# Column bias from raw weight rows on TensorE, a pinned order of loads and splits, and 40 early transposes, in the first pair of a two-block attention kernel

## The chip, the cores and the metric

The kernel runs on one core of one Trainium2 chip. A core has a matrix engine (TensorE, "PE" in the profile, its weight loads "PEld"), three engines for elementwise work (VectorE "DVE", ScalarE "ACT", GpSimd "POOL"), and DMA engines that move data between memory and the core. All transfers of this kernel are issued by SyncE, in whose rows they stand as "SPq" or "SP". Each engine works through a queue of its own in a fixed order, and waits at its head until what it needs is there.

The metric is the device time of one execution, in microseconds (us).

## The reference, cut to what matters

The inputs are x and a context, both (16, 256, 512) in float32, and a boolean mask (16, 256, 256). Two transformer blocks follow one another. Only the first one is touched:

```python
xq  = layer_norm(x, qn_w, qn_b)
ctx = layer_norm(context, cn_w, cn_b)
q  = (xq @ q_w).reshape(B, N, H, D)             # H = 16 heads of D = 32
kv = (ctx @ kv_w).reshape(B, M, 2, H, D)
k, v = (kv[:, :, 0], kv[:, :, 1])
attn = jnp.einsum('bnhd,bmhd->bhnm', q, k) * scale
attn = softmax(where(xa_mask[:, None], neg, attn))
out = jnp.einsum('bhnm,bmhd->bnhd', attn, v).reshape(B, N, C)
x = x + (out @ proj_w + proj_b)
x = x + gelu(layer_norm(x, n2_w, n2_b) @ fc1_w + fc1_b) @ fc2_w + fc2_b
```

The second block is a causal self-attention, a cross-attention over the same context, and an MLP with ReLU, each followed by a layer norm.

A layer norm ahead of a product splits in two: the product of the normalized input with the weights scaled by the gain, and a constant row, offset times weight, which is the bias of that product. This bias is what the first part of the change computes in another way.

## The kernel before

**Tiles.** The 16 batch items go in 8 pairs; a pair has 4 tiles of 128 rows, 512 rows together. Products of the first block's attention use a rounded 32-bit type. To keep float32 accuracy, every operand is split in a high and a low half (`split`, L119: ACT makes the high half by a rounding copy, DVE the difference), and each product is three matmuls (`mm3`, L255): high by high, high by low, low by high.

**The first phase** (`phase1`, L554). For each pair g, `feed(g)` (L679) makes q, k and v. While it does this for pair g, the stream of score products, exponentials, transposes and value products of the pair before is woven in (`weave`, L330). For pair 0 there is nothing to weave with: `feed(0)` runs alone, and the attention of pair 0 starts behind it.

What `feed(0)` does, in its program order:
1. `normal` (L653) loads four tiles of x (`xin`) and normalizes them: DVE's statistics (L238 to L241), POOL's power for the reciprocal deviation `rstd` (L242), DVE's normalization (L247).
2. `cvec` (gains and offsets), `n2` and `b_fc1` (vectors for the later MLP) are loaded, L688 to L690.
3. `load("q")` (L567) loads four 128-row chunks of q_w as raw rows (`wst`), splits each in `q_w_h` and `q_w_l` (L193, L194), and weighs the raw rows: `by_k` is the sum of the chunks, each times its offsets (`weigh`, L216: POOL multiplies the first, ACT scales the others in place at L222, POOL adds them at L223).
4. `front` (L659) transposes each tile by TensorE (`transposed`, L273) and splits it into `x_t`.
5. Four projections `project_t` (L295) give the four 128-column chunks of q. After the first, `shift` (L203) sums `by_k` over its partitions by four matmuls with a column of ones (`sum_cols`, L226) and copies the bias `q_w_b` out of its bank. Each chunk is split with that bias into the tile `qk` (one buffer, `halves`, L539), and `keep` (L375) stores it to a scratch `d` in memory (L378). Between the projections come the fronts of the context, `c_t`, as `FRONTS` says: tiles 0 and 1 after the first, 2 after the second, 3 after the third.
6. The same for k, with `load("k")`, and fronts of pair 1's x between; then `load("v")`, two tiles of v (`values`), v's bias, and `load_o` (L583): proj_w in four chunks, its constant row by the same weighing with v's bias, and `b_o`.

Raw rows and the attention's transposed probabilities share six buffers under the tag "pts". Matmul results use three banks under "mm"; scores use two ("sc"), transposed probabilities two ("pt"), value products one ("z").

**The attention of a pair** begins (`begin`, L604) with the masks: pair 0 loads its own `mk` (`load_mask`, L613) and POOL converts it to `mb` in four instructions (`mask`, L619); it also loads pair 1's. `build` (L383) loads stacks of q and k for four heads from the scratch, `scores` (L404) makes two products for a head and DVE adds mask and row minimum into `e` (L423), ACT exponentiates (L433), and `turn` (L443) transposes `e` three heads later. `residual` (L667) adds the projection of the result to x, which it loads once more (`xr`, L673), together with `b_o`.

**What sets the order.** TensorE's queue keeps the order in which the program is written (L1534). The queues of DVE, ACT, POOL and SP are put in order by a planner: it models when each instruction can run, and may put later-written instructions ahead of earlier ones when data and buffers allow. Therefore the profile shows some loads of `load_o`, `begin` and `residual` among the first ones issued.

Of the kernel before, what the change touches and what calls it, by code (L numbers as in the profile page):

```python
# [20 lines left out]
P = 128  # L21
# [20 lines left out]
def kernel(ctx: ExitStack, tc: tile.TileContext, a, out):  # L42
# [75 lines left out]

    def split(src, dst, bias=None, scale=None):  # L119
# [11 lines left out]
        else:  # L131
            nc.scalar.copy(dst[0], src)
            nc.vector.tensor_tensor(dst[1], src, dst[0].bitcast(F32), ALU.subtract)
# [10 lines left out]
    class Weight:  # L144
# [30 lines left out]
        def load(self, ks, x0=0, n=C):  # L175

            at = slice(x0, x0 + n)
            for k in ks:
                h, l = self.w[0][:, k, at], self.w[1][:, k, at]
                raw = self.stage()  # L180
                nc.sync.dma_start(
                    out=raw, in_=a[self.name][ts(k, P), self.c0 + x0 : self.c0 + x0 + n]
                )
                self.raw[k] = raw
                if self.gain is None:
                    if self.pooled:
                        nc.gpsimd.tensor_copy(h, raw)
                    else:
                        nc.scalar.copy(h, raw)
                    nc.gpsimd.tensor_tensor(out=l, in0=raw, in1=h.bitcast(F32), op=ALU.subtract)  # L190
                else:
                    by = self.gain[:, k : k + 1]
                    nc.scalar.activation(h, raw, AF.Identity, scale=by)  # L193
                    nc.vector.scalar_tensor_tensor(  # L194
                        l, raw, by, h.bitcast(F32), ALU.mult, ALU.subtract
                    )
        def weigh(self, pool):

            self.by_k = None
            for k, raw in self.raw.items():  # L200
                self.by_k = weigh(pool, self.by_k, raw, self.offset[:, k : k + 1])

        def shift(self):  # L203
            by_k = self.by_k
            if self.form == "row":
                self.b = bank("mm", "ps_b")
                nc.tensor.matmul(self.b, ones.to_broadcast([P, P]), by_k, start=True, stop=True)
            else:
                sum_cols(self.b, by_k)
# [5 lines left out]

    def weigh(pool, total, raw, offset):  # L216

        if total is None:
            total = pool.tile([P, 512], F32, tag="by_k", name="by_k", bufs=1)
            nc.gpsimd.tensor_scalar(total, raw, offset, None, ALU.mult)  # L220
        else:
# [332 lines left out]
    def phase1():  # L554
# [124 lines left out]
        def feed(g):  # L679
# [4 lines left out]
            if g < NG:  # L684
# [20 lines left out]
                if g == 0:  # L705
                    load("k")
# [887 lines left out]
```

## Time and profile before

| what | value |
|---|---|
| median of 6 runs | 2814.69 us |
| lowest and highest run | 2807.13 and 2824.4 us |
| profiled execution | 2816.57 us |
| its span, first to last instruction | 2814.9 us |
| mean granted TensorE clock | 0.982 |
| 0 to 110 us: TensorE busy | 89.44 us |
| 110 to 1000 us: TensorE busy | 859.52 us of 890 |

A page shows busy times of each engine and, in tenths, 40 equal slices of the span. A window row gives the length, the busy time of each engine with its count of instructions, the clock granted to TensorE as a share of full speed, the busy share of the DMA engines, and what they moved in GB/s. A timeline row gives start, length, engine, line, operation, result and operands, and a count; the square brackets say how long the engine had been idle before it and what ended that. Lines are those of the kernel before.

### The profile page before, as it was taken

To read this page: it belongs to the slowest core of one execution; us is meant where nothing else is said; L and a number is where in the kernel's file an instruction comes from. 1 tells how busy PE (TensorE), PEld (TensorE's weight loads), DVE (VectorE), ACT (ScalarE), POOL (GpSimd) and SP (SyncE) were. 2 spreads that over 40 slices of the span, in tenths; PEclk is the share of its full clock that TensorE was granted. 3 is DMA by queue.
4 is the path that set the end of the run, shared out by engine and by line. 5 is a ranking of instruction groups with operands and counts; after the bars stand their busy time and mean duration, and the time that the engine had idled before them with its cause. 6 is when DMAs were issued, how large, how long until landed. Compare 5 with 4: busy or idle time off the path is not lost.

```text
span 2814.9 us, 56659 instructions
## 1 busy us (share of the span) xinstructions
PE 2681.3 (95%) x18970; PEld 2263.5 (80%) x18970; DVE 2050.0 (73%) x5763; ACT 1824.2 (65%) x5292; POOL 864.2 (31%) x874
## 2 busy tenths in 40 slices
PE   7999999998899999999999999999999999999998
PEld 5777777776799999898987877777777777777787
DVE  7666666757646559888876777777777777777887
ACT  4877777778455555444447787877777777777532
POOL 6122221204501127666660111114322212213333
PEclk9999999999899999999999999999999999999999
DMA  6566555644323344434366565567665655555221
GB/s 230 173 194 186 168 181 170 195 157 130 131 106 135 121 147 168 150 120 150 120 207 212 187 188 186 183 191 214 207 192 185 181 184 182 183 171 179 97 91 60
DMA packets 287809, 465.41 MB, mean 165 GB/s; under 512 B 36256, under 2 KB 188320, under 8 KB 279328
## 3 DMA queue, kind: packets, MB, share of 16 engines
q1 hardware_dynamic: 287520, 461.78, 51.1%
q8 instruction: 153, 2.51, 0.4%
q14 instruction: 136, 1.11, 0.1%
HBM read 284.97 MB, written 176.69 MB: 164 GB/s over the span
## 4 chain that ended last, share of the span: by engine, by line
PE 68%; DVE 15%; DMA 7%; issue 4%; POOL 3%; ACT 3%; SPq 1%; POOLq 0%; DVEq 0%; ACTq 0%
PE ps_p L258 18%; PE ps_v L258 14%; PE ps_pt L449 9%; PE ps_s L408 5%; PE ps_z L468 5%; PE down L1015 5%; PE up_sc L902 3%; DVE c_t L142 3%; PE up_pt L902 2%; PE up_mm L902 2%; PE ps_t L277 2%; DVE st L238 1%; DMA xd<-x 1%; DVE e L423 1%; ACT e L433 1%
## 5 line engine op out<-in xcount | busy, mean ns | idle before, releaser
L433 ACT ACTIVATE e<-e,mn 128x256 f32<-128x256 f32 (+1 forms) x1024 | 487.6, 481 | 65.2 <-DVE mn L423 62.8
L455 ACT COPY pt<-ps_pt 128x512 f32<-128x512 f32 (+1 forms) x696 | 378.6, 547 | 181.2 <-PE ps_pt L449 167.8
L449 PE MATMUL ps_pt<-ident,e 128*128 128x128 f32 x2816 | 438.3, 274 | 23.0 <-DVE lbias L1255 11.3
L449 PEld LDWEIGHTS ps_pt<-ident,e 128*128 128x128 f32 x2816 | 337.6, 141 | 63.9 <-ACT pt L455 7.7
L408 PE MATMUL ps_s<-stack 97*128 97x256 f32 (+1 forms) x1536 | 332.5, 298 | 17.1 <-ACT e L433 9.7
L408 PEld LDWEIGHTS ps_s<-stack 97*128 97x128 f32 (+1 forms) x1536 | 269.9, 191 | 76.8 <-ACT e L433 17.4
L1322 POOL TENSOR_TENSOR x<-x,zz 128x256 f32<-128x256 f32 x128 | 95.7, 748 | 731.1 <-DVE zz L1315 673.8
L1015 PE MATMUL down<-w_h,c_t 128*128 128x256 f32 x900 | 263.6, 294 | 22.3 <-DVE c_t L142 22.3
L433 ACT ACTIVATE e<-ps_s,mn 128x256 f32<-128x256 f32 x512 | 241.5, 484 | 58.3 <-DVE mn L419 45.7
L1015 PE MATMUL down<-w_h,x_t 128*128 128x256 f32 x868 | 254.2, 293 | 9.6 <-ACT x_t L141 7.3
L1015 PE MATMUL down<-w_l,x_t 128*128 128x256 f32 x868 | 253.0, 291 | 0.0
L423 DVE CUSTOM_DVE_ANT_0 e<-mb,ps_s 128x256 f32<-128x256 bf16 x512 | 193.1, 416 | 81.3 <-PE ps_s L408 78.9
L242 POOL TENSOR_TENSOR rstd<-rstd,nhalf 128x1 f32<-128x1 f32 x192 | 141.3, 741 | 314.4 <-DVE rstd L241 312.9
L258 PE MATMUL ps_p<-x_t,q_h 128*128 128x512 f32 x640 | 215.5, 417 | 4.2 <-DVE qk L128 2.1
L419 DVE TENSOR_REDUCE mn<-ps_s 128x2 f32<-128x512 f32 x256 | 175.1, 684 | 48.5 <-PE ps_s L408 46.3
L468 PE MATMUL ps_z<-pt,v 128*32 128x256 f32 (+1 forms) x3072 | 199.4, 371 | 3.4 <-DVE pt L453 3.3
L1015 PEld LDWEIGHTS down<-w_h,c_t 128*128 128x128 f32 x900 | 180.4, 201 | 25.7 <-DVE c_t L142 25.7
L423 DVE CUSTOM_DVE_ANT_0 e<-tri,ps_s 128x128 f32<-128x128 f32 (+1 forms) x512 | 160.2, 346 | 53.8 <-PE ps_s L408 51.7
L433 ACT ACTIVATION_READ_ACCUMULATOR e<-e,mn 128x1 f32 x1024 | 197.8, 193 | 0.0
L1015 PEld LDWEIGHTS down<-w_h,x_t 128*128 128x128 f32 x868 | 174.6, 201 | 11.3 <-ACT x_t L141 8.8
L141 ACT CAST x_t<-sums 128x512 fp32r<-128x512 f32 x156 | 92.4, 618 | 136.3 <-DVE sums L791 85.8
L1015 PEld LDWEIGHTS down<-w_l,x_t 128*128 128x128 f32 x868 | 174.5, 201 | 0.0
(245 smaller groups left out, 7478.7 us busy)
## 6 DMA issues: line engine op xcount, KB each, us to landing
stack<-d SPq DMA_DIRECT2D x1152, 128.0 KB
d<-qk SPq DMA_DIRECT2D x192, 512.0 KB
hid<-ho SPq DMA_DIRECT2D x32, 1024.0 KB
raw<-hid SPq DMA_DIRECT2D x32, 1024.0 KB
x<-xd SPq DMA_DIRECT2D x128, 256.0 KB
xd<-x SPq DMA_DIRECT2D x96, 256.0 KB
xin<-in_x_dram SPq DMA_DIRECT2D x32, 256.0 KB
xin<-in_ctx_dram SPq DMA_DIRECT2D x32, 256.0 KB
```

The costliest lines, as they stand in the source:

```text
L242: nc.gpsimd.tensor_tensor(out=rstd[:, 1:2], in0=rstd[:, 0:1], in1=nhalf, op=ALU.pow)
L258: nc.tensor.matmul(ps, w[p], x[q], start=(k == 0 and i == 0), stop=(k == kc - 1 and i == 2))
L408: nc.tensor.matmul(ps[:, t, :], u.st[: self.rows, 0, j, ts(t, P)], u.st[: self.rows, 1, j, :], start=True, stop=True,)
L419: nc.vector.tensor_reduce(mn, ps, AX.X, ALU.min)
L423: nc.vector.tensor_tensor_reduce(out=e[:, at], in0=bias[t], in1=ps[:, t, : job.width[t]], scale=-SC, scalar=BIG, op0=ALU.add, op1=ALU.min, ...
L433: nc.scalar.activation(e[:, at], ps[:, t, :] if bias is None else e[:, at], AF.Exp, bias=mn[:, t : t + 1], scale=-1.0, accum_out=u.rs[:, t ...
L449: nc.tensor.transpose(pp[:, ts(x, P)], e[:, at : at + P], ident)
L455: nc.scalar.copy(pt[:, :n], pp[:, :n])
L468: nc.tensor.matmul(z[ts(j, D), w[0] * P :], job.v[u.i * NT + mc][:, u.c * P + j * D : u.c * P + (j + 1) * D], u.pt[j][:, x0 * P : (x0 + le ...
L902: nc.tensor.matmul(ps[:, mm, :], w[p][:, k, :], x[q][:, k, :], start=(first and mm == k == j == 0), stop=(k == 1 and j == 2), skip_group_c ...
L1015: nc.tensor.matmul(ps[:, t, :], x[p][:, mm, ts(t, P)], w[r][:, bo, :], start=(q == mm == t == j == 0), stop=(q == self.NS - 1 and mm == 1 ...
L1322: nc.gpsimd.tensor_tensor(out=xv, in0=xv, in1=zz, op=ALU.add)
```

## The change

It has four parts, all of them in the first phase, and nearly all in what `feed(0)` issues.

- *Transposes of the identity.* 40 transposes of the identity matrix into a bank that nothing uses yet, at the head of TensorE's queue.
- *Bias of q, k and v.* `sum_cols` and the weighing by POOL and ACT are gone. `shift` makes 16 products instead: each 128 by 128 block of raw rows as the stationary operand by the offset column of its chunk, accumulated over the four chunks. They need only the raw rows and `cvec`. For proj_w, whose bias is a row, the weighing stays and is now done by DVE (one multiplication, three multiply-adds).
- *Order of loads and splits of pair 0.* All four chunks of q_w are loaded ahead; the first is split before the fronts of x, the other three only after the last split of x. The fronts of the context are issued only after that and one projection later (tiles 0 and 1 after the second projection, 2 after the third, 3 after the fourth). `load("k")` comes after the last split of x. `load("v")` moves up, from behind the last k projection to behind the first.
- *Loads kept in program order.* For `b_o`, the masks of pairs 0 and 1, and pair 0's `xr`, the planner may no longer issue the load ahead of earlier-written ones. The loads of `n2` and `b_fc1` move from the start of `feed(0)` to `load_o` and are kept there likewise.

As built, TensorE's order changes only by the 40 transposes, the bias products (16 for 4, three times) and the place of the context's transposes. On SP the masks of pair 0 and 1 now stand behind the last chunks of proj_w, `b_o`, `n2` and `b_fc1`. On DVE the four weighing instructions of proj_w stand ahead of the first `e`. On POOL the differences of the last two proj_w chunks stand ahead of the mask conversions.

```diff
@@ split
-            nc.scalar.copy(dst[0], src)
-            nc.vector.tensor_tensor(dst[1], src, dst[0].bitcast(F32), ALU.subtract)
+            latest["h"] = nc.scalar.copy(dst[0], src)
+            latest["l"] = nc.vector.tensor_tensor(dst[1], src, dst[0].bitcast(F32), ALU.subtract)
@@ class Weight
         def load(self, ks, x0=0, n=C):
             for k in ks:
+                self.fetch(k, x0, n)
+                self.part(k, x0, n)
+
+        def fetch(self, k, x0=0, n=C):
+            self.raw[k] = self.stage()
+            nc.sync.dma_start(
+                out=self.raw[k], in_=a[self.name][ts(k, P), self.c0 + x0 : self.c0 + x0 + n]
+            )
+
+        def part(self, k, x0=0, n=C):
...
+                by = self.gain[:, k : k + 1]
+                nc.scalar.activation(h, raw, AF.Identity, scale=by)
+                latest["w"] = nc.vector.scalar_tensor_tensor(
+                    l, raw, by, h.bitcast(F32), ALU.mult, ALU.subtract
+                )
         def weigh(self, pool):
-            self.by_k = None
-            for k, raw in self.raw.items():
-                self.by_k = weigh(pool, self.by_k, raw, self.offset[:, k : k + 1])
+            self.by_k = pool.tile([P, 512], F32, tag="by_k", name="by_k", bufs=1)
+            for k, raw in self.raw.items():
+                by = self.offset[:, k : k + 1]
+                if k == 0:
+                    nc.vector.tensor_scalar(self.by_k, raw, by, None, ALU.mult)
+                else:
+                    nc.vector.scalar_tensor_tensor(
+                        self.by_k, raw, by, self.by_k, ALU.mult, ALU.add
+                    )
         def shift(self):
...
-                sum_cols(self.b, by_k)
+                ps = bank("mm", "ps_b")
+                for c in range(KC):
+                    for k, raw in self.raw.items():
+                        nc.tensor.matmul(
+                            ps[:, c : c + 1],
+                            raw[:, ts(c, P)],
+                            self.offset[:, k : k + 1],
+                            start=(k == 0),
+                            stop=(k == KC - 1),
+                        )
+                nc.vector.tensor_copy(self.b, ps[:, :KC])
-    def weigh(pool, total, raw, offset):
-        if total is None:
-            total = pool.tile([P, 512], F32, tag="by_k", name="by_k", bufs=1)
-            nc.gpsimd.tensor_scalar(total, raw, offset, None, ALU.mult)
-        else:
-            nc.scalar.activation(raw, raw, AF.Identity, scale=offset)
-            nc.gpsimd.tensor_tensor(out=total, in0=total, in1=raw, op=ALU.add)
-        return total
-
-    def sum_cols(b, by_k):
-        ps = bank("mm", "ps_b")
-        for c in range(4):
-            nc.tensor.matmul(ps[:, c : c + 1], by_k[:, ts(c, P)], ones, start=True, stop=True)
-        nc.vector.tensor_copy(b, ps[:, 0:4])
@@ phase1, load_o
-            nc.sync.dma_start(out=w["b_o"], in_=bcast(a["proj_b"], C))
+            tc.keep_in_program_order(
+                nc.sync.dma_start(out=w["b_o"], in_=bcast(a["proj_b"], C))
+            )
+            tc.keep_in_program_order(nc.sync.dma_start(out=n2, in_=a["mlp_vec"]))
+            tc.keep_in_program_order(nc.sync.dma_start(out=b_fc1, in_=a["fc1_b"]))
@@ load_mask
-                nc.sync.dma_start(out=self.mk, in_=of("mask", self.g))
+                load = nc.sync.dma_start(out=self.mk, in_=of("mask", self.g))
+                if self.g < 2:
+                    tc.keep_in_program_order(load)
@@ residual
-                nc.sync.dma_start(out=xr, in_=of("x", g)[:, at, :])
+                load = nc.sync.dma_start(out=xr, in_=of("x", g)[:, at, :])
+                if g == 0:
+                    tc.keep_in_program_order(load)
@@ feed
                 if g == 0:
+                    ps = bank("z", "ps_w")
+                    for i in range(40):
+                        nc.tensor.transpose(ps[:, ts(i % KC, P)], ident, ident)
                     ready = [normal(g, "x_t", t) for t in range(G)]
                     nc.sync.dma_start(out=cvec, in_=a["attn_vec"])
-                    nc.sync.dma_start(out=n2, in_=a["mlp_vec"])
-                    nc.sync.dma_start(out=b_fc1, in_=a["fc1_b"])
-                    load("q")
+                    weight("q")
+                    for k in range(KC):
+                        w["q"].fetch(k)
+                    w["q"].part(0)
                     for t in range(G):
                         yield front(g, "x_t", t, ready[t])()
+                    for k in range(1, KC):
+                        with tc.issue_after(latest["h"].ins), tc.issue_after(latest["l"].ins):
+                            w["q"].part(k)
+                    inputs_split = latest["h"].ins
+                    q_rest = latest["w"].ins
...
-                    for t in FRONTS[c]:
-                        yield front(g, "c_t", t)()
+                    for t in FRONTS[c] if g else ((), (0, 1), (2,), (3,))[c]:
+                        if g == 0:
+                            with tc.issue_after(q_rest):
+                                cost = front(g, "c_t", t)()
+                            yield cost
...
                 if g == 0:
-                    load("k")
+                    with tc.issue_after(inputs_split):
+                        load("k")
                 for c in range(KC):
                     ps = yield from project_t(w["k"].w, c, inputs["c_t"])
                     if g == 0 and c == 0:
                         w["k"].shift()
+                        load("v")
...
-                if g == 0:
-                    load("v")
```

## The prediction

> **What bounds the kernel now.** I read the page's busy times and its 40 slices first, then the busy time in 10 us windows, then the timeline of single engines. The page says that TensorE is the bound almost everywhere and nowhere less than in its first slice, 70 us long:
>
> ```profile
> PE 2681.3 (95%) x18970; PEld 2263.5 (80%) x18970; DVE 2050.0 (73%) x5763; ACT 1824.2 (65%) x5292; POOL 864.2 (31%) x874
> PE   7999999998899999999999999999999999999998
> ```
>
> The change touches only what is issued in the first 105 us or so, so I split that stretch (columns: PE, PEld, DVE, ACT and POOL busy with counts, granted clock, DMA share, GB/s):
>
> ```profile
> 0.00:10.00 10.00, 1.97 (x8) 1.57 (x8) 5.65 (x18) 3.67 (x6) 6.19 (x23) 1.00 0.77 243
> 10.00:20.00 10.00, 5.00 (x14) 3.34 (x15) 10.00 (x18) 7.82 (x14) 7.85 (x9) 1.00 0.82 283
> 20.00:30.00 10.00, 7.76 (x30) 6.11 (x29) 8.50 (x20) 4.65 (x8) 9.57 (x10) 0.85 0.48 160
> 30.00:40.00 10.00, 10.00 (x47) 7.96 (x47) 7.04 (x16) 3.71 (x6) 6.26 (x7) 0.98 0.67 213
> 40.00:50.00 10.00, 6.92 (x29) 5.08 (x28) 6.58 (x14) 4.97 (x8) 7.40 (x7) 0.71 0.75 252
> 50.00:60.00 10.00, 8.58 (x38) 6.48 (x37) 5.62 (x10) 3.35 (x6) 4.62 (x5) 0.95 0.90 284
> 60.00:70.00 10.00, 9.50 (x47) 7.67 (x47) 6.52 (x26) 4.81 (x11) 3.99 (x5) 1.00 0.51 184
> 70.00:80.00 10.00, 9.84 (x67) 7.94 (x67) 3.33 (x19) 10.00 (x36) 2.95 (x3) 1.00 0.42 119
> ```
>
> TensorE works 49.7 of the first 70 us and is full from then on. So what counts is T0, the first score product after v's bias products, and any stall behind it: later work is the same in the same order, and shifts whole. The timeline gives T0 and the points ahead of it:
>
> ```profile
> 9.01 0.43 SPq L615 DMA_DIRECT2D mk<-in_mask_dram  x1
> 13.59 4.11 POOL L619 TENSOR_SCALAR mb<-mk 128x256 bf16<-128x256 uint8 x4
> 18.00 0.79 PE L258 MATMUL ps_p<-x_t,q_w_h 128*128 128x512 f32 x1 [2.30 <-DVE x_t L133]
> 22.85 0.30 PE L230 MATMUL ps_b<-ones,by_k 128*128 128x1 f32 x1
> 40.56 0.69 ACT L122 ACTIVATE qk<-ps_p,q_w_b 128x512 fp32r<-128x512 f32 x1 [1.54 <-DMA d<-qk]
> 65.63 0.95 PE L230 MATMUL ps_b<-ones,by_k 128*128 128x1 f32 x8
> 66.44 0.48 PE L408 MATMUL ps_s<-stack 96*128 96x256 f32 x2
> 69.68 0.33 PE L449 MATMUL ps_pt<-ident,e 128*128 128x128 f32 x1 [0.45 <-ACT e L433]
> ```
>
> T0 is 66.44. Three things are to be seen: the first projection waits for splits (18.00); a projection's split waits until the store of the split before it has landed, since qk has one buffer (40.56); the masks are fetched at 9.01 and converted by 17.70, 49 us before their first use, and cost the attention nothing.
>
> **The change part by part.** *Forty transposes of the identity.* The identity is ready at 1.69 (POOL's 1.40 + 0.29). Eight transposes at 23.98 took 0.94, 0.118 each; the eight at 7.49 took 1.97, some 0.2 each. So 40 take 4.7 to 8 and end at 6.4 to 9.7; the first real transposes start at 7.49. Cost 0 to 2, and I take 0: the first projection waits for DVE's splits well past 9.7. What the change can warm is the clock: products start 0.427 apart at 18.00 to 22.85 and 0.23 apart from 30.75 on. But by the rows TensorE is nearly idle again from 9.5 to 12, so I take no gain (bound: 12 x 0.2 = 2.4).
>
> The Trainium skill, "TensorE: Matmul & The Clock Gate", section "Part 4: PE-mode transpose", says that transposes do not count as TensorE being busy for its clock, which speaks against this part. By it the sum would be the same, since I take no gain; were it wrong, 2.4 us less before the store chain below swallows them. No row here tests it.
>
> *Start of the first projection.* POOL's first by_k (7.73, 1.66 long) stands ahead of the rstd of inputs 3 and 4, and DVE's q_w_l and kv_w_l stand ahead of the last x_t splits (16.61 and 17.29, 0.67 each). Without by_k, rstd comes at about 8.3 and 9.1, xin 3 and 4 (0.54 each) at 9.2 and 10.4, the last x_t cast (0.57) and difference (0.67) at 12.6. Then q_w_l 1 to 3 (0.74 each) end at 14.8, ahead of the products that use them. The first projection runs from 12.1 to 17.2 (12 x 0.427) instead of ending at 22.85: 5.6 earlier.
>
> *Column bias.* Before: eight passes, 65.63 to 66.44, 0.101 each. After: 16 products of two passes, 32 x 0.101 = 3.24, so 2.43 more on TensorE, three times: 7.3. Gone are 3 x 1.66 + 9 x 1.28 = 16.5 of POOL and 9 x 0.7 = 6.3 of ACT. q's bias is there at 17.2 + 3.24 + 0.3 = 20.7 instead of 24.43: 3.7 earlier, and the first q split ends at 22.6 instead of 27.35.
>
> *What the store chain leaves of it.* A round is a split, 40.56 to 42.03 (1.47), and a store, issued 42.06 and landed 45.52 (3.46): 4.9; where loads share the DMA it is longer (store 34.62 to 40.56: 5.9). k's weights are fetched into buffers that q's raw rows free only after q's bias products, at 20.1; SP issues are 0.47 apart and a 256 KB load takes 2.4 from its issue to its user (22.75 to 25.18). So DVE's four kv_w_l and the context splits, pinned behind q's, lie between the rounds. I get the second q split at 29.4 (before 34.27) and the third at 36.2 (before 42.03). k's first products wait for the bank that this frees: 36.6 instead of 38.13. The gain is down to 1.5. They take 3.9 (12 products at 0.23 and the pass-on), then the bias 3.24: 43.8 instead of 43.2. Lost: 0.6.
>
> *From k's bias to T0.* k's first split ends at 45.6 (before 45.07). Its store stands on SP behind four v and proj loads, which wait for k's bias products, and a context load: 5 x 0.47 later, landing at 51. The next split stands on DVE behind an xin whose rstd waits on POOL behind two proj differences (2 x 1.25), and ends at 54.9 (before 54.12). Two rounds of 4.9 more: 64.7. The bias products of v need the bank that this split frees: 64.7 + 3.24 gives T0 = 67.9, 1.5 later. Bounds: TensorE's own work after k's bias (36 k products and 24 v products at 0.23, 16 transposes at 0.1, bias 3.24) is 18.6, so 62.4 is the earliest, 4 gained; rounds as long as before's (45.07 to 65.72, 20.65, after 45.6) give 66.25 + 3.24 and a store delayed once more, 70.2, nearly 4 lost. I take 67.9, built from the single rounds, and keep both ends.
>
> *Masks, b_o, n2, b_fc1 and xr in program order.* Program order puts mk behind load_o. proj 3 and 4 need buffers that v's raw rows hold until the last bias products, so SP issues them at T0 - 0.75, then b_o, n2, b_fc1 and mk: the mask load goes out at T0 + 1.6. The four mask loads of before landed after 4.5, 2.0, 2.2 and 2.7; at 2.8 it lands at T0 + 4.4. POOL has the proj differences 3 and 4 ahead of the conversions: those loads land at about T0 + 2, ACT's casts take 0.7 each, POOL's differences 2 x 1.25, to T0 + 5; then two conversions (4.11 for four, 0.85 the shortest): T0 + 6.7. The first e (0.42) ends at T0 + 7.2. Two score banks exist, so the third score product waits for e; TensorE reaches it at T0 + 1.2. Stall 6.0, where before has 0.45 + 0.16. Bounds: 3.5, if the masks come early, since DVE's by_k of proj 3 and 4 still stands ahead of e; 8, if the mask load lands like the slowest of the four.
>
> The stall comes with a clock price. In before, waits of 1 us in sparse work from 41.0 on brought TensorE to half clock from 44.12 to 50.94 (columns: PE busy, clock, DMA share, GB/s):
>
> ```profile
> 43.00:44.00 1.00, 0.58 (x5) 1.00 1.00 351
> 44.00:45.00 1.00, 0.30 (x3) 0.56 0.67 274
> 49.00:50.00 1.00, 1.00 (x4) 0.50 0.70 84
> 50.00:51.00 1.00, 1.00 (x3) 0.53 0.95 311
> 51.00:52.00 1.00, 1.00 (x7) 1.00 1.02 391
> ```
>
> There the full stretch at half clock lasted from 47 to 50.94 and lost half of itself, 1.7 to 2.0. I add 1.7 (bounds 0 and 3.4). Net: 6.0 - 0.6 + 1.7 = 7.1.
>
> The Trainium skill, same page, section "HAM oscillation — how this bites in real kernels", warns of idle gaps over about 3.4 us. The rows above show half clock after shorter ones, so the measurement is harder than the rule. By the rule a 6 us stall also halves the clock, and a 3.5 us one hardly does.
>
> n2, b_fc1 and the xr loads cost nothing of their own: the first xr add is at 103.2, and the MLP that n2 and b_fc1 serve begins about when the last xr load goes out, at 711.8; without that cover the first residual would wait one landing, 2 to 3 us.
>
> **Sum.** 1.5 + 7.1 = 8.6 on the profiled execution's 2816.57 (span 2814.9 and 1.67 around it): 2825.2. The median of the runs, 2814.69, lies 1.9 below that execution, so 2823.
>
> **The rivals.** *Not slower: the store chain is not what ends last.* Place: k's second split. If TensorE's own work sets T0 (62.4, 4.0 earlier) and the masks, issued with the last proj loads, come at the floor (stall 3.5, net 2.9, no clock price), the sum is -1.1: 2814. It decides from T0 at 63.5 on downwards with that floor, or from 59.3 with the stall I take, which no bound reaches. For it speaks that before's k rounds lay under a DMA share of 0.90; against it, that the order adds loads ahead of that store.
>
> *Worse.* k's first products cold (12 x 0.2 = 2.4), T0 at 70.2 and a stall of 8 with its clock price: 3.8 + 9.1 = 12.9, or 2828. Sparse work at 25 to 36 speaks for it; that POOL has lost 16.5 speaks against it.
>
> *The front gain is kept and the masks are early.* If the wait for qk's buffer goes, T0 falls by the 4.7 of the first split and by the 4.0 above: -8.7, 2806. The row at 40.56 speaks against it.
>
> *No effect.* If nothing of this is on the path: 2815. TensorE's 20 idle us in the first 70 speak against it, but gains and losses may cancel; that lies in the first rival.
>
> **How the numbers follow.** A measurement of this kernel can tell about 0.3%, 8.4 us, from no change. Likeliest, +6 to +12 (2820 to 2827): 0.60, half on either side of 2823.1. Not slower, with no effect in it, -3 to +4: 0.19. Worse, +9 to +18: 0.17. Kept gain: 0.04. Faster 0.04, same 0.30 + 0.19 = 0.49, slower 0.30 + 0.17 = 0.47. The range runs from the first rival's -4 to the worse case's +17: 2811 to 2832; it leaves out the kept gain and the ends of two cases, some 0.1 to 0.15.
>
> **What would show it.** In the changed profile: first projection done near 17 and q_w_b near 21; k's bias products near 40 to 44; T0 at 66 to 70; then one wait of 4 to 8 us of TensorE at the third score product, ended by DVE's e, itself ended by POOL's mb; half clock behind it. Wrong would be: T0 below 63, masks issued before proj 3 and 4, or a change behind 110 us, which this sum doesn't know.

## The result, and the profile after

| | time | over before, 95% interval |
|---|---|---|
| before, median of 63 runs | 2815.68 us | |
| changed, median of 31 runs | 2823.51 us | 1.0029 [1.0022, 1.0036] |
| changed, profiled execution | 2818.49 us (span 2816.8) | |

The change costs 0.29%, about 8 us. The forecast was 2823, in the middle of its likeliest case (2820 to 2827). The total is right. Its steps are not all right, and one profile of each kernel does not add up to it, as will be seen.

First the changed kernel's page (busy times, and TensorE in 40 slices):

```profile
PE 2691.4 (96%) x19082; PEld 2272.0 (81%) x19082; DVE 2044.5 (73%) x5767; ACT 1815.8 (64%) x5280; POOL 840.3 (30%) x858
PE   8999999998799999989989999999999999999998
```

The first slice is fuller than before (8 for 7), and still the kernel is slower: a fuller TensorE is not a gain if it is filled with other work. The windows of the changed kernel show what fills it, in the columns of the table of before:

```profile
0.00:10.00 10.00, 7.94 (x48) 7.70 (x48) 5.04 (x17) 2.92 (x5) 4.49 (x23) 1.00 0.76 256
10.00:20.00 10.00, 7.76 (x38) 6.15 (x39) 9.39 (x20) 4.61 (x8) 1.71 (x3) 0.83 0.35 113
20.00:30.00 10.00, 9.03 (x38) 7.61 (x38) 6.44 (x16) 4.60 (x8) 1.43 (x3) 0.66 0.50 174
30.00:40.00 10.00, 8.47 (x40) 6.59 (x39) 6.84 (x17) 2.39 (x4) 1.61 (x3) 1.00 0.80 253
40.00:50.00 10.00, 10.00 (x57) 8.49 (x55) 4.44 (x10) 3.07 (x5) 0.55 (x1) 0.83 0.66 209
50.00:60.00 10.00, 6.73 (x28) 4.86 (x28) 7.15 (x17) 3.51 (x7) 3.79 (x5) 0.90 0.71 240
60.00:70.00 10.00, 10.00 (x54) 8.63 (x53) 3.83 (x8) 2.44 (x4) 0.95 (x2) 0.93 0.58 204
70.00:80.00 10.00, 3.78 (x21) 3.25 (x21) 5.38 (x14) 3.05 (x9) 5.88 (x6) 0.59 0.34 94
80.00:90.00 10.00, 10.00 (x46) 8.43 (x46) 4.03 (x21) 7.68 (x27) 4.25 (x6) 0.73 0.42 107
```

From 0 to 10 these are mostly the 40 transposes. From 70 to 80, where TensorE was full before, 6 us are empty, and from 80 to 90 the clock stands at 0.73. TensorE's timeline gives the points of the prediction:

```profile
1.75 7.07 PE L710 MATMUL ps_w<-ident 128*128 128x128 f32 x40 [1.75 <-POOL ident masks.py:199]
13.34 0.51 PE L267 MATMUL ps_p<-x_t,q_w_h 128*128 128x512 f32 x1 [0.68 <-ACT x_t L134]
18.10 4.61 PE L228 MATMUL ps_b<-cvec,wst 128*128 128x1 f32 x32
40.96 3.66 PE L228 MATMUL ps_b<-cvec,wst 128*128 128x1 f32 x32
67.53 3.63 PE L228 MATMUL ps_b<-cvec,wst 128*128 128x1 f32 x32
71.02 0.48 PE L417 MATMUL ps_s<-stack 96*128 96x256 f32 x2
72.29 0.63 PE L417 MATMUL ps_s<-stack 96*128 96x256 f32 x2
79.14 0.80 PE L417 MATMUL ps_s<-stack 96*128 96x256 f32 x2 [6.22 <-DVE mn L432]
```

T0 is 71.02 instead of 66.44, and at the third score product TensorE waits 6.22 us. Who holds it stands in the timelines of SP, POOL and DVE of the changed kernel, in order:

```profile
72.82 8.05 SPq L631 DMA_DIRECT2D mk<-in_mask_dram  x2
73.18 2.44 DVE L213 SCALAR_TENSOR_TENSOR by_k<-wst,kv_w_b,by_k 128x512 f32<-128x512 f32 x2 [0.51 <-DMA wst<-in_proj_w_dram]
73.81 2.93 POOL L197 TENSOR_TENSOR proj_w_l<-wst,proj_w_h 128x512 fp32r<-128x512 f32 x2 [9.88 <-DMA wst<-in_proj_w_dram]
76.83 3.63 POOL L637 TENSOR_SCALAR mb<-mk 128x256 bf16<-128x256 uint8 x4
77.72 0.42 DVE L432 CUSTOM_DVE_ANT_0 e<-mb,ps_s 128x256 f32<-128x256 bf16 x1 [2.10 <-POOL mb L637]
```

The mask load goes out at T0 + 1.8. POOL works at the two proj_w differences until 76.74 and then converts; the first e waits for the first conversion, and the score bank for e. (The first of the two loads that the SP row joins is pair 0's; it lands at 76.30.) DVE's weighing of proj_w, which this kernel also has ahead of the first e, ends at 75.62. So three things end within 1.1 us of each other, the weighing, the landing of the mask and POOL's differences, and the masks are the last of them.

The fiftieth product behind T0 starts at 89.12 instead of 76.05, 13.1 later.

**How far one profile carries.** The times of the profiled executions differ by 1.9 us, not by 8. The start of the same instruction in two traces shows where: how much later than in the first profile of before each stretch makes it (us; the stretch of 790 to 1125 adds at most 1.1 in any of them). "Again" are second profiles of the two unchanged kernels, taken with the experiments.

| stretch of before, us | before again | changed | changed again |
|---|---|---|---|
| 0 to 140 | +3.1 | +12.1 | +11.7 |
| 140 to 640 | +2.7 | +5.5 | +6.7 |
| 640 to 790 | +0.4 | -3.1 | -2.3 |
| 1125 to 2600 | +3.5 | -12.7 | -3.6 |

The first 140 us repeat to some 3 us in before and to 0.4 in the changed kernel. The stretch from 1125 on, whose work no part of the change touches, differs by 9 us between two executions of the very same changed kernel. So differences of 5 us and more in the first 140 us are read from profiles here, and the value of a version from its timed runs.

### The profile page after: what moved, and what is told of

It reads as the page before. It is cut to its first block, busy times and chain, and to the rows that moved or that the text cites. A ratio compares the mean times of both kernels' runs of the same rounds, so it can differ in the third digit from the quotient of the medians.

```text
span 2816.8 us, 56853 instructions
## 1 busy us (share of the span) xinstructions
PE 2691.4 (96%) x19082; PEld 2272.0 (81%) x19082; DVE 2044.5 (73%) x5767; ACT 1815.8 (64%) x5280; POOL 840.3 (30%) x858
## 4 chain that ended last, share of the span: by engine, by line
PE 68%; DVE 16%; DMA 6%; issue 4%; POOL 3%; ACT 2%; SPq 0%; POOLq 0%; DVEq 0%; ACTq 0%
PE ps_p L267 18%; PE ps_v L267 14%; PE ps_pt L458 8%; PE ps_s L417 5%; PE ps_z L477 5%; PE down L1050 4%; PE up_sc L937 3%; DVE c_t L144 3%; PE up_pt L937 2%; PE up_mm L937 2%; PE ps_t L286 2%; DVE e L432 1%; DVE st L247 1%; DMA xd<-x 1%; DVE x L261 1%
```

## The experiments

In the table, "k bias" is the start of k's bias products, "product 1000" the start of the thousandth TensorE product behind T0, "wait" the longest idle time of TensorE between T0 and the fiftieth product behind it (a dash: under 1.6). The ratio is over before's runs on the same chip.

| kernel | k bias | T0 | product 1000 | wait | ratio, 95% interval |
|---|---|---|---|---|---|
| before | 42.2 | 66.4 | 215.2 | - | 1 |
| before again | 45.2 | 69.1 | 218.6 | - | |
| changed | 41.0 | 71.0 | 229.1 | 6.22 | 1.0029 [1.0022, 1.0036] |
| changed again | 40.0 | 70.6 | 229.7 | 5.80 | 1.0027 [1.0016, 1.0037] |
| changed, loads free | 46.8 | 75.4 | 226.1 | - | 1.0005 [0.9993, 1.0016] |
| changed, old bias | 47.2 | 66.1 | 214.1 | - | 0.9984 [0.9975, 0.9993] |
| changed, no transposes | 43.1 | 72.5 | 228.9 | 5.65 | 1.0017 [1.0008, 1.0026] |
| changed, early mask | 39.2 | 68.5 | 219.7 | - | 0.9995 [0.9983, 1.0006] |
| changed, mixed bias | 46.3 | 68.1 | 219.5 | - | 0.9980 [0.9968, 0.9991] |
| changed, early mask and v | 45.2 | 70.7 | 220.6 | - | 0.9972 [0.9961, 0.9984] |
| before, only new bias | 43.2 | 73.3 | 222.8 | - | 0.9996 [0.9987, 1.0005] |
| before, only kept loads | 41.0 | 65.6 | 216.7 | - | 1.0016 [1.0005, 1.0027] |
| before, only new order | 51.2 | 73.8 | 223.9 | - | 0.9999 [0.9986, 1.0012] |
| before, only transposes | 42.9 | 66.6 | 217.0 | - | 0.9989 [0.9978, 1.0001] |

The theory: the loss has two places, T0 (bias products on TensorE and what the store chain makes of the front) and the wait for the masks behind T0. The rivals: the wait only looks like the masks', and DVE's weighing of proj_w would hold e anyway; or the kept loads, the order or the transposes cost by themselves.

### Before, unchanged, profiled once more

> The kernel before, unchanged, profiled once more: how much of the differences between two profiles is chance. If the first 215 us repeat within 2 us (T0 at 66.4, the thousandth product behind it at 215.2), then differences there of 7 to 14 us are those of the kernels; behind 1265 us I expect differences of some us either way between two executions of the same kernel, as its runs differ by up to 17 us.

T0 came 2.6 later and product 1000 3.4 later, more than the 2 us expected, and 7.4 more were lost behind it. This sets the grain: a T0 that differs by 3 tells nothing, a wait of 6 us does.

### All loads free again

```diff
-            tc.keep_in_program_order(nc.sync.dma_start(out=w["b_o"], in_=bcast(a["proj_b"], C)))
-            tc.keep_in_program_order(nc.sync.dma_start(out=n2, in_=a["mlp_vec"]))
-            tc.keep_in_program_order(nc.sync.dma_start(out=b_fc1, in_=a["fc1_b"]))
+            nc.sync.dma_start(out=w["b_o"], in_=bcast(a["proj_b"], C))
...
-                if self.g < 2:
-                    tc.keep_in_program_order(load)
...
-                if g == 0:
-                    tc.keep_in_program_order(load)
...
+                    nc.sync.dma_start(out=n2, in_=a["mlp_vec"])
+                    nc.sync.dma_start(out=b_fc1, in_=a["fc1_b"])
```

> The changed kernel with only its fourth part undone: no load is kept in program order, and the loads of n2 and b_fc1 stand at the start again. As built, the masks of pairs 0 and 1 go out right after the first weights. Theory of two prices (T0 4.6 later, and 8.5 more lost between T0 and the fiftieth product behind it, by the wait for the masks and the half clock after it): T0 stays near 71, the 6.2 us wait at the third score product falls below 1.5, the fiftieth product behind T0 comes about 10 us after it instead of 18.1, and the time is 8 lower: about 2815. Rival (the wait only changes its owner: DVE's weighing of the last two proj_w chunks, which need v's bias products too, holds the first e): a wait of 3 to 4 us stays, about 2820. Rival (what decides is only T0): 2823.

The wait is gone, as the theory has it, and DVE did not hold e: the planner now puts the weighing of proj_w between the e. The ratio fell by 0.0024, 7 us. But T0 did not stay at 71: it went to 75.4. The masks, b_o and xr go out between the first weights and the context again. In the window of 10 to 20 us the DMA share of this kernel is

```profile
10.00:20.00 10.00, 7.85 (x39) 6.18 (x39) 8.79 (x18) 4.45 (x8) 4.61 (x5) 0.83 0.65 233
```

0.65 against 0.35 in the changed kernel. k's first products then wait on a context split that this kernel's DVE has behind a late load of pair 1's x:

```profile
41.91 0.79 PE L267 MATMUL ps_p<-c_t,kv_w_h 128*128 128x512 f32 x1 [2.52 <-DVE c_t L135]
```

So keeping loads back did something for the front, in this order of the rest, while it made the wait. That the early loads are the cause of the later T0 is likely by these rows but not tried alone.

### Only the mask moved forward

```diff
             def begin(self):
-                if self.g == 0:
-                    self.load_mask()
-                    for t in range(G):
-                        self.mask(t)
...
                         w["k"].shift()
                         load("v")
+                        job.load_mask()
+                        for t in range(G):
+                            job.mask(t)
```

> The changed kernel with one move: the load of pair 0's mask and its four conversions are written behind the load of v's weights, ahead of proj_w, and everything else stays pinned. As built, SP issues the mask ahead of proj_w 1 and 2, and POOL converts it ahead of the proj differences; DVE's weighing of proj_w 3 and 4 still stands near the first e. Theory that the masks make the wait at the third score product: T0 stays at 70 to 72, the wait falls from 6.2 to at most 3.5, the time is 4 to 8 under the changed kernel's, so 1.0000 to 1.0015 of before. Rival (the proj weighing on DVE holds e anyway): the wait stays above 4.5, no more than 2 gained.

This is the run that decides. One load and four conversions are written earlier, and everything else is as changed. The rows of SP, POOL, TensorE and DVE:

```profile
43.63 0.45 SPq L627 DMA_DIRECT2D mk<-in_mask_dram  x1
48.37 4.16 POOL L633 TENSOR_SCALAR mb<-mk 128x256 bf16<-128x256 uint8 x4 [7.78 <-DMA mk<-in_mask_dram]
68.46 0.48 PE L417 MATMUL ps_s<-stack 96*128 96x256 f32 x2
69.98 1.06 PE L417 MATMUL ps_s<-stack 96*128 96x256 f32 x4
69.24 0.41 DVE L432 CUSTOM_DVE_ANT_0 e<-mb,ps_s 128x256 f32<-128x256 bf16 x1
```

The masks are converted 16 us before T0, e starts 0.8 after T0, and the third score product has no wait. From T0 to the fiftieth product behind it this run takes 10.2 us, where the changed kernel takes 18.1: 7.9 less. Product 1000 is 9.4 earlier; most of the rest is T0, 2.6 earlier than in the changed kernel, which by the repeat of before can be chance. The ratio is 0.0034 lower, 9.6 us, and the intervals do not touch (their near ends are 4.5 us apart). So this move gives back as much as the change loses.

It moved more than the masks, though. POOL's differences now stand behind the conversions, as written, and the planner has put DVE's weighing between the e, so the rival's 3 to 4 us for the weighing (the prediction's floor of 3.5) do not come. What early masks are worth with the weighing left ahead of e was not run. By the changed kernel's rows DVE was free 2.1 us before its first e, so an estimate is that some 4 of the 6.2 us would have stayed.

### The old bias in the changed kernel

```diff
-                for c in range(KC):
-                    for k, raw in self.raw.items():
-                        nc.tensor.matmul(
-                            ps[:, c : c + 1], raw[:, ts(c, P)], self.offset[:, k : k + 1],
-                            start=(k == 0), stop=(k == KC - 1),
-                        )
+                for c in range(KC):
+                    nc.tensor.matmul(ps[:, c : c + 1], self.by_k[:, ts(c, P)], ones, start=True, stop=True)
...
-                    nc.vector.tensor_scalar(self.by_k, raw, by, None, ALU.mult)
+                    nc.gpsimd.tensor_scalar(self.by_k, raw, by, None, ALU.mult)
...
-                    nc.vector.scalar_tensor_tensor(self.by_k, raw, by, self.by_k, ALU.mult, ALU.add)
+                    nc.scalar.activation(raw, raw, AF.Identity, scale=by)
+                    nc.gpsimd.tensor_tensor(out=self.by_k, in0=self.by_k, in1=raw, op=ALU.add)
...
             w[n].load(range(KC))
+            w[n].weigh(pool)
```

> The changed kernel with only its second part undone: by_k is summed by POOL and ACT again, for proj_w too, and the column bias takes 4 products with the column of ones instead of 16. As a consequence raw buffers come free earlier, and as built SP issues the last proj_w chunks and the masks before the second k store. Theory that the bias products are the price (3 x 2.85 on TensorE and half clock behind them, and late masks because raw rows are held until v's bias products): T0 falls from 71.0 to 60 to 65, no wait over 1.5 us at the third score product, 2808 to 2814. Rival (the chain of stores and splits sets T0, and POOL's by_k delays the norms again): T0 at 66 to 71, 2814 to 2820.

T0 is 66.1, the lower end of the rival's 66 to 71; the wait is gone, as the theory has it: raw buffers come free by POOL and ACT, and the mask goes out at 53.6. The time is 0.16% under before's. The rival's mechanism is in the trace, too: q's bias has to wait for POOL.

```profile
23.55 1.87 PE L226 MATMUL ps_b<-ones,by_k 128*128 128x1 f32 x8 [4.80 <-POOL by_k L214]
```

So the same kept loads cost a 6 us wait with the new bias and none with the old. It is the pair that loses: raw rows held until v's products, and masks queued behind the last loads that need those rows' buffers.

### The new bias alone

```diff
-                sum_cols(self.b, by_k)
+                ps = bank("mm", "ps_b")
+                for c in range(KC):
+                    for k, raw in self.raw.items():
+                        nc.tensor.matmul(
+                            ps[:, c : c + 1], raw[:, ts(c, P)], self.offset[:, k : k + 1],
+                            start=(k == 0), stop=(k == KC - 1),
+                        )
+                nc.vector.tensor_copy(self.b, ps[:, :KC])
...
-            w[n].weigh(pool)
```

> The kernel before with only the column bias of q, k and v by 16 products from raw rows; proj_w's row is weighed by POOL and ACT as before, the planner places loads freely, the masks go out at the start. Theory that the products are paid on TensorE (2.85 a group, three groups, and half clock for some us behind each): T0 at 73 to 77 instead of 66.4, 2821 to 2826. Rival (TensorE has 20 idle us ahead of T0, so they fill gaps, and the freed POOL and ACT bring the norms forward): T0 at 63 to 68, 2811 to 2817.

T0 came at 73.3, as the theory said, but the time did not follow: 0.9996, the rival's number. Product 1000 is 7.6 and 4.2 later than in the two profiles of before. In this profile 5.1 us come back at the start of the MLP (640 to 790). TensorE's idle time there is 3.2 less than in before. Of this 1.9 lies where TensorE waits 6.6 us ahead of transposes of the MLP's inputs in both profiles of before and both of the changed kernel, and here 1.35 and 3.32. That the planner ordered something else there is likely but not shown. A later T0 thus need not cost its length.

### Without the transposes, and only the transposes

```diff
-                    ps = bank("z", "ps_w")
-                    for i in range(40):
-                        nc.tensor.transpose(ps[:, ts(i % KC, P)], ident, ident)
```

> The changed kernel without the 40 transposes of the identity. In the changed kernel they hold TensorE until 8.8, and the first real transposes start 1.2 us later than before, at full clock. Theory that the later store chain swallows what happens there: T0 within 1.5 of 71.0, time within 2 of 2823.5. Rival (the warm clock is worth its 1 to 2 us on the way to T0): 2825. Rival (they only delay): 2821.5.

The wait stays (5.65), T0 is 72.5, product 1000 within 0.8 of the changed kernel's. The same three lines added to before:

> The kernel before with only the first part, the 40 transposes of the identity. Theory (they hold up the first real transposes by 1.2 us, warm a clock that is cold again before the projections, and the store chain swallows either): 0.9993 to 1.0007 of before, T0 within 3 of 66 to 69. Rival (clock kept, the first projection at 0.23 instead of 0.427 a product): T0 2 lower, 0.999 or less.

In this kernel the first projection began at 18.9 instead of 14.9 and T0 was 66.6: the front's start is swallowed on the way. 1.0017 against 1.0029 and 1.0027, and 0.9989 against 1, are too near for a verdict: each interval touches what it is compared with, and the two point opposite ways.

### Only the kept loads

```diff
+                if self.g < 2:
+                    tc.keep_in_program_order(load)
...
+            tc.keep_in_program_order(nc.sync.dma_start(out=n2, in_=a["mlp_vec"]))
+            tc.keep_in_program_order(nc.sync.dma_start(out=b_fc1, in_=a["fc1_b"]))
```

(b_o and pair 0's xr likewise, and the two loads at the start taken out.)

> The kernel before with only the fourth part: masks of pairs 0 and 1, b_o and pair 0's xr kept in program order, n2 and b_fc1 moved to load_o and kept. As built, the raw buffers come free by POOL's and ACT's weighing, so proj_w 3 and 4, b_o and the masks go out right after the first k store, and POOL converts before T0. Theory (keeping the order costs only where raw rows are held until v's bias products): no wait for masks, T0 within 2 of 66.4, time within 3 of before's; it may gain, as fewer early loads compete. Rival (keeping the order is itself the loss): a wait of 3 us or more behind T0, 4 or more slower.

No wait, T0 at 65.6, as expected: with the old bias the mask goes out at 50.2. But the time is 0.16% over before's, 4.5 us, more than the 3 allowed and the size that the rival named, though its wait did not come. Product 1000 (216.7) lies between before's two, and 7.5 us of this execution's loss stand behind 2010, in work that is the same. Where the median's 4.5 come from stays open.

### Only the order

The edit: the third part of the change in the kernel before, without transposes, kept loads or new bias.

> The kernel before with only the third part, the order of loads, fronts and splits: no transposes of the identity, bias by by_k and 4 products, no load kept in program order. With the old bias and the transposes and the kept loads this order gave 0.9984 of before. Theory (the order gains at the front what the store chain then hands on in part): first projection 2 or more earlier than before's 14.9 to 22.8, T0 64 to 67, 0.998 to 1.000. Rival (without the kept loads it crowds the DMA, as in the run with all loads free, whose T0 was 75.4): T0 at 70 or more, 1.001 or above.

The first projection starts at 13.5, but its bias waits for POOL, which now has the mask conversions ahead of by_k:

```profile
28.52 1.86 PE L226 MATMUL ps_b<-ones,by_k 128*128 128x1 f32 x8 [9.26 <-POOL by_k L214]
```

T0 is 73.8, the rival's number, and yet the ratio is 0.9999, the theory's. Again 5.3 us come back between 640 and 790. Both expectations tied T0 to the time more closely than this kernel does.

### Two mixtures

The first keeps the 16 products for q only and lets POOL and ACT sum by_k for k and v:

```diff
             w[n].load(range(KC))
+            w[n].weigh(pool, nc.gpsimd)
```

> The changed kernel, with q's bias from raw rows as it is, but k's and v's bias by by_k, summed by POOL and ACT, and 4 products each; proj_w weighed by DVE; transposes, order and pins as changed. Theory that the k and v products and the held raw rows are the price, while q's come where nothing else could run: k's bias products near 41 as in the changed kernel, T0 at 60 to 63, masks converted before it, no wait over 2 at the third score product: 5 to 8 under before's time. Rival (POOL's by_k puts the norms late again, as it did with the old bias): T0 at 65 to 67, 0 to 3 under before's.

0.9980, 5 to 6 us faster than before, as the theory said, but T0, at 68.1, was above even the rival's 65 to 67: k's first products waited 3.72 us for the third q split. The second combines the early mask with by_k for v alone:

```diff
             w[n].load(range(KC))
+            if n == "v":
+                w[n].weigh(pool, nc.gpsimd)
...
                         load("v")
+                        job.load_mask()
+                        for t in range(G):
+                            job.mask(t)
```

> The changed kernel with pair 0's mask written ahead of proj_w, as in the run with the early mask, and v's bias alone by by_k, summed by POOL and ACT, and 4 products; q's and k's stay with 16 products. Theory (v's products lie directly on the way to T0, and their cooling behind it): T0 2 to 4 below the 68.5 of that run, no wait behind it, 0.9965 to 0.9985 of before. Rival (POOL's by_k of v holds back the norms of the context, or the planner reorders something later): T0 not below 67, 0.999 to 1.001.

It has the lowest ratio, though its interval overlaps those of the mixed and the old bias: 2815.4 us where before had 2822.2 and the changed kernel 2830.1 on the same chip, 0.28% under before and 0.5% under the changed kernel. T0, at 70.7, is again the rival's. v's bias is short once more, while k's bias comes 4 to 5 us later (45.21) than in the changed kernel: an rstd at 38.37 stands on POOL behind an addition of v's by_k (36.88, 1.53), and the normalization and context split that k's first products wait for (2.04 us) stand behind it. Half clock from 41.3 to 44.7 adds up to 1.7.

```profile
45.21 4.18 PE L238 MATMUL ps_b<-cvec,wst 128*128 128x1 f32 x32
69.88 0.95 PE L233 MATMUL ps_b<-ones,by_k 128*128 128x1 f32 x8
70.69 0.48 PE L427 MATMUL ps_s<-stack 96*128 96x256 f32 x2
```

Against the changed kernel product 1000 is 8.5 to 9 earlier, which is about the missing wait with its half clock. Against before it is 2.0 and 5.5 later in its one profile, and 3.0 come back between 640 and 790; its gain over before is a result of the timed runs whose place is not found.

### The changed kernel again

> The changed kernel, unchanged, on the same chip as the three beside it, and profiled once more. It should repeat 1.0022 to 1.0036 of before, T0 at 71 within 3, and the wait of 5.5 to 7 us at the third score product.

It repeats: T0 70.6, and the wait

```profile
78.86 0.80 PE L417 MATMUL ps_s<-stack 96*128 96x256 f32 x2 [5.80 <-DVE mn L432]
```

## Why the prediction was right, and which of its terms were not

- **Transposes** (cost 0, end at 6.4 to 9.7): they end at 8.8, and the first real ones start at 8.65, 1.2 late. Taking them away or adding them alone gave no clear difference. Right as far as the runs can tell. (The "eight transposes at 23.98" are the row of their weight loads; the products start at 24.09, 0.11 apart, which changes nothing in the sum.)
- **First projection** (12.1 to 17.2): 13.34 to 18.10, 4.7 earlier than before, 0.9 short of the forecast. Without the transposes it started at 13.1 as well, so they are not what it waited for.
- **Column bias** (3.24 a group): the groups take 4.47, 3.52 and 3.49 to the next product. Passes are 0.112 apart; the 0.101 was an eighth of a group whose first two passes are 0.03 apart. And q's group fell to half clock in its middle. That last is a term the prediction did not have.
- **Store chain**: the q splits end at 24.4, 32.2 and 37.6 (forecast 22.6, 29.4, 36.2), k's first products start at 37.72 (36.6) and its bias ends at 44.6 (43.8). Most of the lead of 4.7 was gone there, as said.
- **From k's bias to T0** (67.9, bounds 62.4 and 70.2): 71.02 and 70.57, over the upper bound. This is the step that was mis-sized. The first k split ended at 46.3 (45.6), the second at 57.0 (54.9), since the store of the first, issued at 46.85 behind four weight loads and a context load, landed at 54.3, 7.4 later; I had 51. From 57.0 on TensorE has no gap, and its own work sets T0: twelve k products partly at half clock, 24 v products and 3.5 of bias. The reason I gave, that v's bias waits for a bank, does not show in the trace: those products follow v's without a gap.
- **Masks** (stall 6.0): 6.22 and 5.80. The mask load went out at T0 + 1.8 (1.6), POOL's differences ended at T0 + 5.7 (5.0), the second conversion at T0 + 7.6 (6.7). Right in every part, with the landing 0.9 later than forecast (76.30, T0 + 5.3), and the run with the early mask shows the cause. The floor of 3.5 took it that DVE's weighing stays ahead of e; in the run with the loads free and in that with the early mask the planner moved it.
- **Half clock behind the stall** (1.7, bounds 0 and 3.4): the clock was half from 71.7 to about 85.3, of which 79.1 to 85.3 was work, 3.1 lost. But it fell ahead of the stall, behind v's products, and the early-mask run has 3.4 us of it without any stall, so it is not the stall's alone. The stretch of before from which the 1.7 was taken holds not only waits of 1 us but also k's eight one-column passes (42.18 to 43.20), and does not tell the two apart.
- **Sum**: 13.1 at the fiftieth product where 8.6 was forecast, and 7.8 in the medians. The step to T0 was 3.1 too small and the clock behind the stall 1.4. That the total was hit all the same is in part luck: the timed runs lost some 4 us less than the first 140 us of both profiles (12.1 and 11.7). Part of that may come back between 640 and 790 (-3.1 and -2.3 in the two profiles, +0.4 in the second of before), while 140 to 640 loses more (+5.5 and +6.7, where the second of before has +2.7). So the sign of being wrong that the prediction named, a change behind 110 us, is there in part; the rest lies within what two executions of one kernel differ by, and is not settled.
- **Rivals**: "not slower" did not come, since T0 would have had to be 63.5. "Worse" had T0 at 70.2, near the measured one, and a total 4 to 5 us too high. That T0 was no good measure of the time, none of the four cases foresaw: with the new bias alone and with the order alone it came 4 to 7 later than in before's two profiles, at an unchanged time.

## What to carry to other kernels

When a load is pinned in program order, look for what stands ahead of it on its queue and which buffer that waits for: here a 6 us wait came from masks behind weight loads that needed buffers whose raw rows a new consumer held longer. Writing that load and its conversions earlier gave back what four changes had lost, and one combination with it measured 0.28% under before. Where two profiles of one kernel differ by 3 us at a point and by 10 in a late stretch, only timed runs tell a version's worth; the profile tells which wait has appeared.

## What the runs showed of the hardware

- **One-column products let the clock fall.** TensorE works without a gap through q's bias, and its granted clock halves in the middle of it (changed kernel, TensorE busy, clock, DMA share, GB/s):

```profile
18.00:20.00 2.00, 2.00 (x20) 1.00 0.04 8
20.00:22.00 2.00, 2.00 (x14) 0.63 0.00 0
22.00:24.00 2.00, 2.00 (x8) 0.50 0.64 221
24.00:26.00 2.00, 2.00 (x6) 0.50 1.01 354
26.00:28.00 2.00, 2.00 (x9) 0.66 0.52 211
```

  The passes are 0.112 apart until 20.47 and 0.214 apart after; the projection behind them runs at 0.427 a product until 27. By the same kind of rows it was half from 44.4 to 47.8 behind k's group, and from 71.7 on behind v's. The kernels compare: in the six profiles where v's bias takes 32 passes, the clock falls to half between 0.6 us before and 0.7 us after T0. In the eight where it takes 8, it falls 2.8 and 3.1 us after T0 in two and not within 8 us of it in the others. So a group of 32 such passes costs more than its own 3.5 us: half of the stretch from 20.5 to 27.4 for q's, 3.4, of which 1.0 lies in the group itself.
- **These transposes raised it.** The 40 transposes start 0.213 apart until 6.71 and 0.109 apart from 6.91 on, 5.2 us after the first, and the eight real ones at 8.65 follow at 0.11 each. (The window rows give a clock of 1.00 there all along, and in before until 20 us, because the profile records the clock only from 6.9 and from 23.6 on; ahead of that the spacing tells, as the 0.427 a product at 18.00 in before does.) The Trainium skill, "TensorE: Matmul & The Clock Gate", section "Part 4: PE-mode transpose", says that the full clock does not engage for TensorE's transpose mode, as it doesn't count as busy in the same way. For these float32 transposes against an identity the runs differ: the first change of clock that the profile records comes at 4.8 to 7.4 us in the eight profiles with the 40 transposes and at 18.0 to 24.0 in the six without. The measurement decides; whether they use the mode that the page means, no run here shows. The warmth did not last: after two short groups of transposes at 10.4 and 12.0 the first projection ran at 0.43 a product.
- **Half clock lasted through an idle stretch and for 6 us of work after it.** In the changed kernel:

```profile
78.00:80.00 2.00, 0.86 (x3) 0.50 0.00 0
80.00:82.00 2.00, 2.00 (x8) 0.50 0.23 53
82.00:84.00 2.00, 2.00 (x9) 0.50 0.53 153
84.00:86.00 2.00, 2.00 (x9) 0.66 0.78 185
86.00:88.00 2.00, 2.00 (x14) 1.00 0.54 136
```

  The clock had fallen at 71.7, ahead of the wait, which began at 72.9. In the early-mask run, where TensorE has no wait there, it was half from 68.9 to 72.3 only. The wait of 6.2 us and the half of 79.1 to 85.3 that was lost are 9.3; against the early-mask run, which pays some half clock too, the difference is the 7.9 told above.
